# Two chains of pieces in the first stage, and a few input products of a 256-state scan moved from GpSimd to VectorE

## The chip, the core and the metric

The kernel runs on one core of a Trainium2 chip. The core has five engines, each with its own instruction queue that is worked off in order: TensorE (PE; its weight loads are listed as PEld), VectorE (DVE), ScalarE (ACT), GpSimd (POOL) and SyncE (SP), whose queue issues nearly all the DMA transfers here. Engines wait for each other through semaphores. All compute engines reach the on-chip memory SBUF; matrix products are written to PSUM, which DVE and ACT also read and write, and POOL does not use here. The metric is the device time of one execution in microseconds (us), lower is better.

## The reference

Four images of 128 channels and 64 x 64 pixels, all in float32, go through three parts.

1. *Ordering and a 16-state scan.* A group normalisation, then two depthwise 3 x 3 convolutions with Gelu and a channel gate between them give a score for each 4 x 4 patch; the 4096 pixels of each image are sorted by patch score. A selective scan with 256 channels of 16 states runs over the sorted pixels, and its result is put back in image order and added to the image.
2. *A 256-state scan.* Over the 4096 tokens of each image, with 256 channels `d` and 256 states `n`:

```python
deltaA = jnp.exp(jnp.einsum('bld,dn->bldn', delta, A))
deltaB = jnp.einsum('bld,bln->bldn', delta, Bv)
def step(state, inp):
    dA_i, dB_i, x_i, C_i = inp
    state = dA_i * state + dB_i * x_i[:, None, :]
    y = jnp.einsum('bdn,bn->bd', state, C_i)
    return (state, y)
```

3. *Spectral filters.* Causal convolutions of each image's tokens with 16 filters (in a plus and a minus form), each followed by a 128 x 128 matrix, plus a short autoregressive term. The matrices are sums over four branches, weighted by a softmax and by powers of `sigma`.

## The kernel before

The program has three stages in time: `layer0_front` (the ordering, until about 608 us), `layer0_scan` (the 16-state scan, until about 2850 us) and `layer1` (the 256-state scan with the spectral filters beside it, to the end).

**First stage, `layer0_front`.** A loop over the four images `b` (L118). For each: load the image into `xs`, take its statistics (L126), normalise it into the bordered tile `xg` (L144), copy it by patches into `xp1` (L149), transpose it in eight groups of four with statistics of each token (L164 to L172), take the powers `rs` and `r1` on POOL (L142, L176), and normalise the tokens `x1` on ACT (L183, 32 instructions). I call this the token part. Then the ordering part: the first convolution with Gelu (eight calls of `conv`: four of its nine taps are matmuls at L104, five are instructions on DVE at L106, of which the first reads PSUM and the others read only SBUF), the channel gate (L198 to L211), the second convolution (L215), scores (L225), ranks and the permutation matrix (L243 to L264), and the reordered tokens as matmuls with that matrix (L274, L277), stored to `xnt` (L278). `xs`, `xg`, `x1` and `f1` have one buffer each; `xp1` and the second convolution's result `f2` share one under the tag `patches`. Beside this the generator `spectral_weights` makes the spectral matrices: a softmax on the weights, the matrices `mue` from `M_u`, and then for each of 16 filters a load, four scalings on ACT (L677), three sums on POOL (L679) and two combinations on POOL (L695, L696), and stores. The loop advances it six times for each image but the first. In this stage the order of instructions on each engine is not the order in which the program emits them: a planner goes by emission as a priority and takes what is ready by its own estimate of time.

**Second stage, `layer0_scan`.** It is not touched. Its operations serve as prices: POOL forms inputs of 1024 elements per partition (L491), DVE scans them (L513) and multiplies the states, which lie in PSUM, by a tile in SBUF (L517).

**Third stage, `layer1`.** Here the order of instructions is written out by hand. There are 32 parts: four images of eight chunks of 512 tokens (`TS`). A part is 256 steps of the loop over `k` (L1253), one step for one channel `d`. States lie on the partitions, in two halves, so a step works on 128 x 1024 elements. Step `k` issues, in this order:

- `fetch` for step k + 8, every second step: delta of two channels, spread over all partitions by a DMA into `dlb` (L1140);
- `carry` for step k + 10, every 128 steps: two small products or sums on POOL (L1149, L1150) that bring in the state of the chunk before;
- `spread` for step k + 4, every second step (`VD` = 2 channels): POOL multiplies `u` by delta for both channels and writes tile `v` (L1155, three buffers); ACT puts in the first column (L1159);
- `lift` for step k + 1: ACT writes the decay factors as two exponentials into one of two PSUM tiles `da` (L1164);
- `scan` of step k: DVE's scan instruction over `da` and `v`, into `s` (L1167);
- every eight steps (`GD`) the list of six pieces of `contract`, of which one is taken at each of the next six steps: matmuls of the states with C into the PSUM tile `yp` (L1184) and ACT's copies out of it (L1190);
- one piece of the side work `beside` (the output of the part before, and the projections of the part after). A piece of kind `mm` (matmuls into `middle()`) is taken only at step 6 of eight and its evacuation (`post`) at step 7. `middle()` and `yp` share a single PSUM buffer, of which the eight steps are the timetable;
- spectral convolutions on PE up to a fixed number of columns per step (L1113, L1055), with ACT's copies (L1125).

Of the kernel before, what the change touches and what calls it, by code (L numbers as in the profile page):

```python
# [15 lines left out]
NB = 4  # L16
L = 4096
# [6 lines left out]
def layer0_front(ctx: ExitStack, tc, ident, half, w, x, xnt, perm_t, pqd, mud):  # L24
# [9 lines left out]
    pm = ctx.enter_context(tc.tile_pool(name="a_pm", bufs=4, space=PSUM))  # L34
# [83 lines left out]
    for b in range(NB):  # L118

        xs = xp.tile([128, L], F32, tag="xs", name="xs")  # L120
        nc.sync.dma_start(xs, x[b])
        for _ in range(6 if b else 0):
            next(matrices, None)
# [4 lines left out]
        nc.vector.bn_aggr(mv, st)  # L128

# [12 lines left out]
        nc.gpsimd.tensor_tensor(rs, sq, half[:, 0:1], ALU.pow)  # L142
        xg, inside = bordered("xg")
# [3 lines left out]
        xp1 = xp.tile([128, L], F32, tag="patches", name="xp1")  # L147
        for oy in range(4):
            nc.scalar.copy(  # L149
                by_patch(xp1, oy), inside[:, oy::4, :].rearrange("c py (px ox) -> c py px ox", ox=4)  # L150
            )


        x1 = xp.tile([128, 2, 16, 128], F32, tag="x1", name="x1")
# [5 lines left out]
        for h in range(2):  # L160
            for oy in range(4):
                tp = pm.tile([128, 4, 128], F32, tag="mm", name="tp")
                for ox in range(4):
                    nc.tensor.transpose(tp[:, ox, :], patches[:, h, 4 * oy + ox, :], ident)  # L164
                o4 = bass.ts(oy, 4)
                nc.vector.tensor_tensor(x1[:, h, o4, :], tp, pe[:, h, o4, :], ALU.add)
                for o in range(4):
                    nc.vector.bn_stats(stx[:, h, 4 * oy + o, :], tp[:, o, :])
                    nc.vector.bn_stats(st1[:, h, 4 * oy + o, :], x1[:, h, 4 * oy + o, :])
            for o in range(16):  # L170
                nc.vector.bn_aggr(mvx[:, h, o, :], stx[:, h, o, :])
                nc.vector.bn_aggr(mv1[:, h, o, :], st1[:, h, o, :])  # L172
# [8 lines left out]
        for h in range(2):  # L181
            for o in range(16):
                nc.scalar.activation(  # L183
                    x1[:, h, o, :], x1[:, h, o, :], AF.Identity, bias=m1[:, h, o : o + 1],
                    scale=r1[:, h, o : o + 1],
                )
# [4 lines left out]
        for i in range(8):  # L191
            h, oy = divmod(i, 4)
            nc.scalar.activation(
                inside1[:, 32 * h + oy : 32 * h + oy + 29 : 4, :], conv(xg, d1, w1, h, oy), AF.Gelu, bias=b1,
                accum_out=sums[:, i : i + 1],
            )
        mean = sm.tile([128, 1], F32, tag="mean", name="mean")
# [9 lines left out]
        nc.scalar.activation(ca, cap, AF.Sigmoid)  # L207
        d2b = xp.tile([128, PT, 128], F32, tag="d2b", name="d2b")
# [3 lines left out]
        f2 = xp.tile([128, L], F32, tag="patches", name="f2")  # L212
        for i in range(8):
# [4 lines left out]
            )  # L218

# [3 lines left out]
        for h in range(2):  # L223
            for o in range(16):
                nc.tensor.matmul(  # L225
                    sc[:, h, o : o + 1], fpatch[:, h, o, :], head,
                    start=True, stop=True,
                )
        s1 = sm.tile([128, 2, 16], F32, tag="s1", name="s1")
# [8 lines left out]

# [9 lines left out]
        for h in range(2):  # L248
# [10 lines left out]
            nc.vector.tensor_scalar(perm[:, h, :], index, more, None, ALU.is_equal)  # L259
        for h in range(2):  # L260
# [3 lines left out]
            nc.vector.tensor_copy(perm_t[:, b, h, :], tp.rearrange("p k j -> p (k j)"))  # L264


        xn = xp.tile([128, 3 + L], F32, tag="xn", name="xn")
        nc.vector.memset(xn[:, 0:3], 0.0)
        ranked = xn[:, 3:].rearrange("c (r o) -> c o r", o=16)
        for o in range(0, 16, 2):  # L270
# [6 lines left out]
            nc.scalar.activation(ranked[:, o : o + 2, :], ps, AF.Identity, bias=nb, scale=ng)  # L277
        nc.sync.dma_start(xnt[b], xn)  # L278

# [346 lines left out]
def spectral_weights(ctx, tc, sigma, m_u, m_plus, m_minus, log_w, gumbel, pqd, mud):  # L626
# [21 lines left out]
    tot = cp.tile([128, 1], F32, name="tot")  # L648
    nc.scalar.activation(soft, lw, AF.Exp, accum_out=tot)
# [31 lines left out]
    mu = mp.tile([128, 4, 3, 128], F32, name="mu", bufs=1)  # L681
    for i in range(4):
        nc.sync.dma_start(mu[:, i], m_u[i].rearrange("k d e -> d k e"))
    mue = mp.tile([128, 4, 3, 128], F32, name="mue", bufs=1)
    branch_sums(lambda r: mue[:, r], lambda i: mu[:, i], lambda i: wt[:, i : i + 1])
    nc.sync.dma_start(mud, mue)
    yield
    for k in range(NK):
        raw = mp.tile([128, 2, 4, 128], F32, tag="raw", name="raw")
        nc.sync.dma_start(raw[:, 0], m_plus[:, k].rearrange("i d e -> d i e"))  # L690
        nc.sync.dma_start(raw[:, 1], m_minus[:, k].rearrange("i d e -> d i e"))
        sums = mp.tile([128, 2, 4, 128], F32, tag="sums", name="sums")
# [23 lines left out]
def layer1(ctx: ExitStack, tc, ident, half, weights, phi, pqd, mud, x, omd, permd, x2, x3, out):  # L716
# [435 lines left out]
    def spread(d, dl, ready):  # L1152
# [3 lines left out]
            v[:, :, :, 1:], ready[0][:, :, 1:].unsqueeze(1).broadcast_to((128, VD, 2, TS - 1)),  # L1156
            dl[:, :, 1:].unsqueeze(2).broadcast_to((128, VD, 2, TS - 1)), ALU.mult,
        )
        nc.scalar.copy(v[:, :, :, 0], ready[5][:, :, bass.ds(d, VD)].rearrange("p h d -> p d h"))  # L1159
        return v  # L1160

# [66 lines left out]
    side, kind = None, None  # L1228
# [24 lines left out]
    for k in range(-10, steps):  # L1253
# [8 lines left out]
        if 0 <= j < steps and j % VD == 0:  # L1262
            vs[j // VD] = spread(j % 256, dls[j // VD], ready[j // 256])
# [21 lines left out]
        if kind == "free" or (kind == "mm" and at_step == 6) or (kind == "post" and at_step == 7):  # L1285
            kind = next(side, None)
        if at_step == GD - 1:
# [100 lines left out]
```

## Time and profile before

| what | us |
| --- | --- |
| three runs | 21599.78, 21605.29 (median), 21611.06 |
| profiled execution, its own time | 21607.92 |
| span of that execution, first to last instruction | 21606.2 |
| first stage, to the issue of the last `xnt` store | 607.7 |
| third stage, first scan to end | about 2859 to 21606 |

In the page's groups a line gives source line, engine, operation, output and inputs, partitions x elements, count, then busy time and the mean in ns of one, then idle time of the engine just before these instructions and what ended it. The chain of waits runs back from the last instruction to what released each one. Consecutive instructions of DVE or POOL overlap by some tens of nanoseconds when the next one waits for nothing, so that the distance between starts is a little shorter than a duration. A chunk of the third stage is 256 scans; counted from the first scan of one to the first of the next it takes 576 to 583 us. POOL's, DVE's and ACT's busy time in the stretch from 2880 to 21540 us are 18503.58, 18308.82 and 14178.81.

### The profile page before, as it was taken

What the parts mean: (1) busy time and instruction counts of PE and PEld (TensorE: products, weight loads), DVE (VectorE), ACT (ScalarE), POOL (GpSimd) and SP (SyncE); (2) the same over time, 40 slices, a digit from 0 to 9 for tenths busy, and PEclk for the clock granted to TensorE, in tenths of its full rate; (3) what the DMA queues carried; (4) which work ended last, traced back from release to release, by engine and by line L of the source; (5) the groups of instructions that cost most, each with busy time, mean ns of one, the idle gap of its engine ahead of it and who ended that gap; (6) DMA issues with size and microseconds to landing.
All of it is one profiled execution on the core that took longest, in us unless ns stands there. A gap on an engine that the chain in (4) does not pass through costs nothing.

```text
span 21606.2 us, 294251 instructions
## 1 busy us (share of the span) xinstructions
PE 17698.4 (82%) x99308; PEld 7770.7 (36%) x99308; DVE 20631.8 (95%) x11807; ACT 16015.2 (74%) x29548; POOL 20268.9 (94%) x5679
## 2 busy tenths in 40 slices
PE   6788854564858888886858999599999999999997
PEld 3344421231323333342323344243434434334434
DVE  6788889999999999999999999999999999999996
ACT  3677767777777777777777777787877777788875
POOL 2677789999999999999999999999999999999996
PEclk7999976676979999997979999699999999999999
DMA  1455544554656776665656777577777777777776
GB/s 68 112 140 140 140 150 151 170 181 160 216 173 218 219 222 218 220 214 186 211 178 218 227 236 235 169 236 232 236 230 228 232 232 231 231 231 229 228 229 187
DMA packets 2497355, 4302.23 MB, mean 199 GB/s; under 512 B 803256, under 2 KB 1320160, under 8 KB 2492768
## 3 DMA queue, kind: packets, MB, share of 16 engines
q1 hardware_dynamic: 2495840, 4283.40, 63.9%
q8 instruction: 784, 12.85, 0.2%
q14 instruction: 731, 5.99, 0.1%
HBM read 3658.98 MB, written 623.38 MB: 198 GB/s over the span
## 4 chain that ended last, share of the span: by engine, by line
DVE 47%; POOL 22%; PE 13%; ACT 8%; issue 6%; DMA 3%; SPq 0%; DVEq 0%; POOLq 0%; ACTq 0%
DVE s L1167 40%; POOL v L1155 21%; PE conv L1113 5%; ACT da L1164 5%; DVE states L513 3%; PE yp L1184 2%; DVE p L517 1%; PE fin L1055 1%; ACT f L505 1%; DMA dlb<-delta 1%; PE y L529 1%; DMA strip<-in_phi 1%; PE mm L422 1%; DMA yd<-ye 0%; PE conv L104 0%
## 5 line engine op out<-in xcount | busy, mean ns | idle before, releaser
L1155 POOL TENSOR_TENSOR v<-u,dlb 128x2044 f32<-128x2044 f32 x4096 | 18381.6, 4552 | 78.1 <-DMA dlb<-delta 68.3
L1167 DVE TENSOR_TENSOR_SCAN s<-da,v 128x1024 f32<-128x1024 f32 x8192 | 18134.6, 2272 | 249.2 <-ACT da L1164 124.8
L1164 ACT ACTIVATE da<-dlb,at 128x511 f32<-128x511 f32 x16384 | 11303.8, 690 | 2143.1 <-DVE s L1167 1688.3
L1113 PE MATMUL conv<-strip,tok 128*128 128x512 f32 (+3 forms) x20480 | 8656.1, 550 | 59.3 <-DMA strip<-in_phi 58.9
L1184 PE MATMUL yp<-s,c 128*32 128x256 f32 x65536 | 4952.4, 431 | 2709.5 <-DVE s L1167 1432.2
L1113 PEld LDWEIGHTS conv<-strip,tok 128*128 128x128 f32 x20480 | 3676.8, 192 | 4144.2 <-issue 3708.3
L1184 PEld LDWEIGHTS yp<-s,c 128*32 128x32 f32 x65536 | 1963.0, 120 | 6485.6 <-issue 1834.3
L1159 ACT COPY v<-vf 128x4 f32<-128x4 f32 x4096 | 814.6, 199 | 2128.6 <-DVE s L1167 2098.4
L1055 PE MATMUL fin<-conved,pq 128*128 128x512 f32 (+1 forms) x3968 | 1799.7, 546 | 16.2 <-ACT sum L1076 8.9
L491 POOL TENSOR_TENSOR v<-dx,bcb 128x1024 f32<-128x1024 f32 x512 | 1207.2, 2358 | 431.2 <-DVE states L513 427.0
L513 DVE TENSOR_TENSOR_SCAN states<-f,v 128x1024 f32<-128x1024 f32 x512 | 1175.9, 2297 | 175.9 <-ACT f L505 126.1
L505 ACT ACTIVATE f<-dt,an 128x255 f32<-128x255 f32 x2048 | 973.6, 476 | 420.9 <-DVE states L513 370.2
L1190 ACT COPY ye<-yp 128x512 f32<-128x512 f32 x2048 | 1185.9, 579 | 27.0 <-PE yp L1184 26.2
L1125 ACT COPY conved<-conv 128x512 f32<-128x512 f32 (+1 forms) x1728 | 986.6, 571 | 213.8 <-PE conv L1113 212.1
L529 PE MATMUL y<-p,ident 128*128 128x512 f32 x2048 | 1005.8, 620 | 154.2 <-DVE p L517 149.2
L1055 PEld LDWEIGHTS fin<-conved,pq 128*128 128x128 f32 x3968 | 669.8, 194 | 394.8 <-issue 284.0
L517 DVE TENSOR_TENSOR p<-states,bcb 128x1024 f32<-128x1024 f32 x512 | 627.0, 1225 | 39.3 <-PE y L529 0.5
L529 PEld LDWEIGHTS y<-p,ident 128*128 128x128 f32 x2048 | 368.8, 195 | 685.4 <-issue 356.0
L422 PE MATMUL mm<-ow,yg 128*32 128x128 f32 x2048 | 278.1, 294 | 107.0 <-ACT om L426 105.3
L422 PEld LDWEIGHTS mm<-ow,yg 128*32 128x32 f32 x2048 | 233.8, 138 | 212.0 <-ACT om L426 128.4
L356 PE MATMUL mm<-xin,taps 128*128 128x512 f32 x512 | 237.6, 608 | 27.2 <-issue 13.8
L398 POOL TENSOR_TENSOR e<-e,e 128x1024 f32<-128x1024 f32 x32 | 75.1, 2346 | 186.3 <-DMA bcb<-bcd 150.6
(240 smaller groups left out, 5851.1 us busy)
## 6 DMA issues: line engine op xcount, KB each, us to landing
dlb<-delta SPq DMA_DIRECT2D x4096, 512.0 KB, 4.1
strip<-in_phi SPq DMA_DIRECT2D x1536, 448.0 KB, 4.7
yd<-ye SPq DMA_DIRECT2D x2048, 256.0 KB, 4.0
strip<-in_phi SPq DMA_DIRECT2D x1088, 256.0 KB, 4.3
bcb<-bcd SPq DMA_DIRECT2D x1024, 256.0 KB, 4.1
pq<-pqd SPq DMA_DIRECT2D x1472, 64.0 KB, 3.7
yt<-yd SPq DMA_DIRECT2D x4096, 4.0 KB, 3.4
pq<-pqd SPq DMA_DIRECT2D x256, 128.0 KB, 3.8
```

Of the source, the lines that this page charges most:

```text
L491: nc.gpsimd.tensor_tensor(v, ready[n][2][:, :, bass.ts(i, SUB)].unsqueeze(1).broadcast_to((128, 2, 2, SUB)), bc[:, 0].unsqueeze(2).broadca ...
L505: nc.scalar.activation(factors[j % 2][:, a, k, 1:], ready[n][1][:, k, SUB * i + 1 : SUB * i + SUB], AF.Exp, scale=an[:, k, 2 * g + a : 2 * ...
L513: nc.vector.tensor_tensor_scan(states.rearrange(flat), factors[j % 2].rearrange(flat), v.rearrange(flat), 0.0, ALU.mult, ALU.add)
L529: nc.tensor.matmul(t.rearrange("p k t -> p (k t)"), ident, p[:, a].rearrange("p k t -> p (k t)"), start=g == 0 and a == 0, stop=False, ski ...
L1055: nc.tensor.matmul(fin[:, bass.ds(c0, w)], pq[:, n, :], u[:, bass.ds(c0, w)], start=begin and n == 0, stop=end and not partly, skip_group_ ...
L1113: nc.tensor.matmul(ps[:, skip:], tok[:, 1 - r if side else r, j, :], strip[:, bass.ds(c0 - lo, TS - skip)], start=which == 0 and j == js[0 ...
L1125: nc.scalar.copy(u[:, cols], ps[:, cols])
L1155: nc.gpsimd.tensor_tensor(v[:, :, :, 1:], ready[0][:, :, 1:].unsqueeze(1).broadcast_to((128, VD, 2, TS - 1)), dl[:, :, 1:].unsqueeze(2).br ...
L1164: nc.scalar.activation(da[:, h, 1:], dl[:, d % VD, 1:], AF.Exp, scale=at[:, h, d : d + 1])
L1167: nc.vector.tensor_tensor_scan(s[:, d % GD].rearrange("p h t -> p (h t)"), da.rearrange("p h t -> p (h t)"), v[:, d % VD].rearrange("p h t ...
L1184: nc.tensor.matmul(yp[i // 2][bass.ts(q, 32), i % 2], c[:, h, t], s[:, :, h, t], start=h == 0, stop=h == 1)
L1190: nc.scalar.copy(ye, yp[j].rearrange("p i d t -> p i t d"))
```

## The change

*First stage.* The loop body is split into two generators, `tokens(b)` (the token part, returning `xg`, `x1` and small tiles) and `ordered(b, ...)` (the rest, with the normalisation of `x1` in eight pieces of four instructions after each piece of the first convolution). A driver emits the tokens of image 0, and then for each image pieces of its ordering in turn with pieces of the tokens of the next image and steps of the spectral matrices: five steps of those for each image. `xp1` and `f2` have a buffer each, `x1` has two, `xn` takes the buffer of `xs`, and the PSUM pool of convolutions and transposes has six buffers in place of four. `spectral_weights` pauses before the softmax, handles `M_u` in three pieces by lag in place of one tile, and fetches the matrices of one filter ahead.

*Third stage.* At steps 118 and 246 of each part (`k % 128 == 118`), `spread` has POOL form only the first of the two channels. A new generator `relief` makes the other: at step 6 of eight ACT copies its delta from `dlb` into `middle()`, a PSUM tile, and at step 7, after that step's scan, DVE multiplies `u` by it into `v` (128 x 2 x 511 elements). A side piece of kind `mm` that would stand at that step 6 waits for the next group of eight.

```diff
-    pm = ctx.enter_context(tc.tile_pool(name="a_pm", bufs=4, space=PSUM))
+    pm = ctx.enter_context(tc.tile_pool(name="a_pm", bufs=6, space=PSUM))
...
-    for b in range(NB):
-        xs = xp.tile([128, L], F32, tag="xs", name="xs")
+    def tokens(b):
+        xs = xp.tile([128, 3 + L], F32, tag="xs", name="xs")[:, 0:L]
         nc.sync.dma_start(xs, x[b])
-        for _ in range(6 if b else 0):
-            next(matrices, None)
+        yield
...
-        xp1 = xp.tile([128, L], F32, tag="patches", name="xp1")
+        xp1 = xp.tile([128, L], F32, tag="xp1", name="xp1")
...
-        x1 = xp.tile([128, 2, 16, 128], F32, tag="x1", name="x1")
+        x1 = xp.tile([128, 2, 16, 128], F32, tag="x1", name="x1", bufs=2)
...
-        for h in range(2):
-            for o in range(16):
-                nc.scalar.activation(
-                    x1[:, h, o, :], x1[:, h, o, :], AF.Identity, bias=m1[:, h, o : o + 1],
-                    scale=r1[:, h, o : o + 1],
-                )
+        return xg, x1, mvx, r1, m1
+
+    def ordered(b, xg, x1, mvx, r1, m1):
...
+            for o in range(4 * i, 4 * i + 4):
+                h, o = divmod(o, 16)
+                nc.scalar.activation(
+                    x1[:, h, o, :], x1[:, h, o, :], AF.Identity, bias=m1[:, h, o : o + 1],
+                    scale=r1[:, h, o : o + 1],
+                )
+            yield
...
-        f2 = xp.tile([128, L], F32, tag="patches", name="f2")
+        f2 = xp.tile([128, L], F32, tag="f2", name="f2")
...
-        xn = xp.tile([128, 3 + L], F32, tag="xn", name="xn")
+        xn = xp.tile([128, 3 + L], F32, tag="xs", name="xn")
...
+    first = Pieces(tokens(0))
+    first.go()
+    for b in range(NB):
+        rest = Pieces(ordered(b, *first.result))
+        first = Pieces(tokens(b + 1)) if b + 1 < NB else Pieces(iter(()))
+        first.go(1)
+        for _ in range(4):
+            rest.go(2)
+            next(matrices, None)
+        first.go(1)
+        rest.go(2)
+        first.go(1)
+        rest.go(4)
+        first.go(1)
+        next(matrices, None)
+        rest.go(6)
+        for n in (1, 1, 1, 1, 1, 1, 2, 2):
+            first.go(1)
+            rest.go(n)
+        first.go()
+        rest.go()
...
+    for k in range(3):
+        raw = mp.tile([128, 2, 4, 128], F32, tag="raw", name="mu")[:, 0]
+        nc.sync.dma_start(raw, m_u[:, k].rearrange("i d e -> d i e"))
+        sums = mp.tile([128, 2, 4, 128], F32, tag="sums", name="mue")[:, 0]
+        branch_sums(lambda r: sums[:, r], lambda i: raw[:, i], lambda i: wt[:, i : i + 1])
+        nc.sync.dma_start(mud[:, :, k], sums)
...
+    ahead = fetch(0)
+    yield
+    for k in range(NK):
+        raw, ahead = ahead, fetch(k + 1) if k + 1 < NK else None
...
-    def spread(d, dl, ready):
+    def spread(d, dl, ready, n):
         v = wk.tile([128, VD, 2, TS], F32, tag="v", name="v", bufs=3)
         nc.gpsimd.tensor_tensor(
-            v[:, :, :, 1:], ready[0][:, :, 1:].unsqueeze(1).broadcast_to((128, VD, 2, TS - 1)),
-            dl[:, :, 1:].unsqueeze(2).broadcast_to((128, VD, 2, TS - 1)), ALU.mult,
+            v[:, 0:n, :, 1:], ready[0][:, :, 1:].unsqueeze(1).broadcast_to((128, n, 2, TS - 1)),
+            dl[:, 0:n, 1:].unsqueeze(2).broadcast_to((128, n, 2, TS - 1)), ALU.mult,
         )
...
+    def relief(v, dl, ready):
+        ps = middle()
+        nc.scalar.copy(ps, dl[:, VD - 1, :])
+        yield
+        nc.vector.tensor_tensor(
+            v[:, VD - 1, :, 1:], ready[0][:, :, 1:], ps[:, 1:].unsqueeze(1).broadcast_to((128, 2, TS - 1)),
+            ALU.mult,
+        )
+        yield
...
-            vs[j // VD] = spread(j % 256, dls[j // VD], ready[j // 256])
+            mine = k % 128 == 118 and kind != "post"
+            vs[j // VD] = spread(j % 256, dls[j // VD], ready[j // 256], VD - mine)
+            if mine:
+                helping = relief(vs[j // VD], dls[j // VD], ready[j // 256])
...
-        if kind == "free" or (kind == "mm" and at_step == 6) or (kind == "post" and at_step == 7):
+        if kind == "free" or (kind == "mm" and at_step == 6 and not helping) or (kind == "post" and at_step == 7):
             kind = next(side, None)
+        if helping and at_step >= 6:
+            next(helping)
+            helping = helping if at_step == 6 else None
```

## The prediction

> **What bounds the kernel now.** I read the page's shares and its chain of waits first, then the groups, then busy time by stage, then order in time inside one stage.
>
> ```profile
> PE 17698.4 (82%) x99308; PEld 7770.7 (36%) x99308; DVE 20631.8 (95%) x11807; ACT 16015.2 (74%) x29548; POOL 20268.9 (94%) x5679
> DVE 47%; POOL 22%; PE 13%; ACT 8%; issue 6%; DMA 3%; SPq 0%; DVEq 0%; POOLq 0%; ACTq 0%
> L1155 POOL TENSOR_TENSOR v<-u,dlb 128x2044 f32<-128x2044 f32 x4096 | 18381.6, 4552 | 78.1 <-DMA dlb<-delta 68.3
> L1167 DVE TENSOR_TENSOR_SCAN s<-da,v 128x1024 f32<-128x1024 f32 x8192 | 18134.6, 2272 | 249.2 <-ACT da L1164 124.8
> L491 POOL TENSOR_TENSOR v<-dx,bcb 128x1024 f32<-128x1024 f32 x512 | 1207.2, 2358 | 431.2 <-DVE states L513 427.0
> L517 DVE TENSOR_TENSOR p<-states,bcb 128x1024 f32<-128x1024 f32 x512 | 627.0, 1225 | 39.3 <-PE y L529 0.5
> ```
>
> DVE and POOL look equally busy, and the chain runs through both. The rows of stretches part them (columns: stretch, length, then PE, PEld, DVE, ACT and POOL busy, clock, DMA share, GB/s).
>
> ```profile
> 60.00:200.00 140.00, 80.51 (x239) 50.31 (x237) 98.19 (x130) 67.55 (x138) 96.67 (x83) 0.72 0.36 118
> 200.00:335.00 135.00, 100.31 (x306) 61.17 (x306) 92.41 (x268) 44.16 (x76) 6.00 (x2) 0.81 0.08 32
> 7494.00:8073.00 579.00, 505.09 (x2920) 204.68 (x2924) 573.11 (x285) 432.11 (x798) 578.77 (x136) 0.98 0.71 221
> 2880.00:21540.00 18660.00, 15426.81 (x92198) 6618.99 (x92191) 18308.82 (x9039) 14178.81 (x26210) 18503.58 (x4329) 0.91 0.68 212
> ```
>
> In a chunk of the 256-state scan (third row, 256 steps in 579 us) POOL works 578.77 us: it never rests. The instructions of DVE in order of time show what its 573 hides:
>
> ```profile
> 12168.59 0.67 DVE L927 TENSOR_TENSOR t<-mm,t 128x512 f32<-128x512 f32 x1
> 12169.17 17.55 DVE L1167 TENSOR_TENSOR_SCAN s<-da,v 128x1024 f32<-128x1024 f32 x8
> 12205.30 19.73 DVE L1167 TENSOR_TENSOR_SCAN s<-da,v 128x1024 f32<-128x1024 f32 x9
> 12241.76 53.89 DVE L1167 TENSOR_TENSOR_SCAN s<-da,v 128x1024 f32<-128x1024 f32 x24 [0.43 <-POOL v L1155]
> ```
>
> Nine scans with inputs in stock take 19.73 us, so (19.73 - 2.27) / 8 = 2.18 us a step. The 24 that follow POOL take (53.89 - 2.27) / 23 = 2.244, which is POOL's pace: 18381.6 / 4096 / 2 = 2.244. Back-to-back scans overlap; waiting ones lose that, and busy time cannot see it. So POOL is the bound here, and DVE's own need per chunk is 256 x 2.1825 = 558.7, plus its small work. L927 starts 0.58 us before the next scan although it lasts 0.67: seven such (4.1), two groups of eight statistics instructions (12224.95 to 12225.99 on the same timeline, 2.1 together) and four of L880 (0.28 each, 1.0), 7.2 in all, plus ACT's 124.8 / 32 = 3.9. Together 569.8, some 10 us under POOL.
>
> In the first stage no engine is full (second row above: PE 100, DVE 92 of 135 us): a chain binds it.
>
> ```profile
> 54.36 5.45 POOL r L176
> 228.53 5.45 POOL r L176
> 363.17 5.45 POOL r L176
> 499.41 5.41 POOL r L176
> 607.68 8.01 DMA xnt<-xn
> ```
>
> L176 stands near the end of an image's token part. Its distances are 174.2, 134.6 and 136.2 us, and after the last, 108.3 us to the final store. So ordering an image alone takes 108, and 27 us of each period are the next image's tokens in series. The first period has 39 more: the chain there runs through L677, L679, L695 and L696, the spectral matrices (POOL busy 96.67 of 140).
>
> **The change, part by part.**
>
> Spreads. 64 of 4096 lose half. POOL's full one steps by 4.488 us. The half is bounded by 2.24 (half) and 2.36 (L491, 1024 elements); I take 2.29, nearer the second since that row has the size. Saved: 2.2 x 2 = 4.4 us a chunk. POOL's need falls from 579.9 (128 x 4.488 = 574.4, L1149/L1150 twice 1.5, L787/L788 twice 1.24) to 575.5.
>
> The product on DVE. 1022 elements, one operand in PSUM like L517 (1.225, less the 0.09 overlap that L927 shows: 1.14). Upper bound: if it shared a port with POOL it would stretch as the two-SBUF-operand instructions did in the first image:
>
> ```profile
> L106 DVE SCALAR_TENSOR_TENSOR sum<-f,w2b,sum 128x512 f32<-128x512 f32 x32 | 41.2, 1299 | 0.8
> L106 DVE SCALAR_TENSOR_TENSOR sum<-f,w2b,conv 128x512 f32<-128x512 f32 x8 | 5.9, 737 | 9.0 <-PE conv L104 6.1 <-ACT f L215 2.9
> ```
>
> While POOL worked (60 to 200 us), the SBUF-only form took 1299 ns (750 in the second image) but the form with an operand in PSUM 737. The new product is of the second kind: 1.14, with 2.6 as its bound. DVE's need: 569.8 + 2.3 = 572.1, under POOL's 575.5; at 2.6 it is 575.0, level. So POOL stays the bound and each chunk falls by 4.4: 32 x 4.4 = 141. I take off half a microsecond a chunk (16), because DVE's reserve shrinks from 10 to 3.4 us: after the relief POOL leads by 4.36 + 1.14 - 1.5 (carry, same step) - 2.29 = 1.7 us, and with three v buffers it must stop at about one pair, 4.4; a statistics group (1.04) or ACT hold-up can add up to that. **Third stage: -125**, bounds -141 and 0.
>
> A rule that speaks against this: the Trainium skill (Perfetto Trace Analysis, Identifying the Most-Contended Engine) takes the engine of highest occupancy as the bottleneck. By it DVE, 95% to 94%, is the bound and the change loads it with 64 x 1.14 = 73 us, which would be the sum for this stage. The step of 2.18 against 2.244 overrules it for me.
>
> ACT's copy of delta into PSUM: 64 x 0.58 (L1190, same size) = 37 us, beside ACT's idle (14179 busy of 18660); its price without that cover is those 37. The added wait: the product waits for that copy. Behind it on DVE stand scan 120 and all later; PE's yp of the next group waits for it too (one PSUM buffer), ACT's exponentials for the scan. The copy stands behind two exponentials (1.38), perhaps a conved copy (0.57) and 0.2 for the v column: done some 2.7 us after scan 117, while DVE reaches the product after two scans, 4.36. No wait, 1.6 us in hand.
>
> The matmul piece that gives up its slot comes 8 steps (18 us) later. The projection ends (last L882) some 437 us into a chunk of 580, so this is hidden; uncovered it would be 18 us a chunk.
>
> First stage. The tokens of images 1 to 3 move beside the ordering of the image before: up to 3 x 27 = 81. DVE has room: 92.4 busy of 135, its gaps lying under the score matmuls and the ranked ones (13.66 and 14.41 on the chain of the last image) and the gate. The normalisation L183, 12.43 us in front of the first Gelu on that chain, is cut into eights between Gelus: up to 10 per image, though DVE, then nearly full, returns most; I count 9 in all. More PSUM and x1 buffers only make this possible. The matrices stay in series with image 0: their instructions were emitted with images 1 to 3 and yet ran at 76 to 180 us, so where they are emitted hardly sets when they run. If they do spread, up to 39 more; then the two-operand L106 of other images stretch instead, which gives part back. **First stage: -90**, bounds 0 and -150.
>
> SP's queue: the M_u loads and store become three of each, same bytes; matrix loads go one ahead; xs now shares its buffer with xn, so an image's load waits for a store: 8.0 + 9.2 (median landing) = 17 us, against the first convolution's 27 us of DVE work (40 x 0.67) before it is needed. Without that cover, 17 us for each of two images. POOL's two powers (0.56 and 5.4) can stand behind a matrix (6.4): 6 us late on a token chain of 27 within 108. The added pause before the softmax moves 103 us of POOL work that has the whole stage.
>
> **Sum.** The profiled run is 21607.9 (span 21606.2): - 125 - 90 = 21393. The median is 2.6 lower: 21390.
>
> **Rivals.**
> - In-order queues keep the tokens in series (for: DVE's statistics wait for transposes, which would queue behind PE's convolution matmuls; against: PE idles 35 of 135 us). Third stage only: 21605 - 125 = 21480.
> - The product waits for POOL's half of the same tile: 1.5 + 2.29 = 3.8 more per event, DVE 569.8 + 2 x 4.9 = 579.6 per chunk, and the relief is worth nothing: 21605 - 90 = 21515. Against: different columns. For: tile v is shared by three engines.
> - The matrices spread and L183 hides: -150 - 125: 21330.
> - Slower: the wait for ACT's copy, at scan 120. To eat the first stage's 90 us a chunk must reach 582.7, so (582.7 - 569.8) / 2 = 6.5 us per event, a wait of 5.3. ACT's longest recorded wait for PE in this stage is 4.1 us (conved), less 1.6 in hand: 2.5. If every wait were 8 us: 569.8 + 2 x 9.1 = 588, +8.2 x 32 - 90: 21777.
> - It does nothing measurable: both rivals one and two: 21605.
>
> **How the numbers follow.** Forecast 0.58 (own range 21350 to 21440), tokens in series 0.12, wait for POOL 0.10, everything better 0.12, slower 0.05, nothing 0.03. A measurement of this kernel tells about 0.2% (43 us) from no change. Faster 0.92, same 0.03, slower 0.05. The range 21325 to 21515 leaves out the last two cases and the far end of the better one.
>
> **What will show it.** Right: a chunk of about 576 us with POOL still without rest; 64 DVE products near 1.2 us with no gap before them; L176 distances near 110 us after the first and the final xnt store near 520. Wrong: a gap ahead of the product ended by POOL or ACT; POOL idle, ended by DVE; half spreads well above 2.4; L176 distances still 135.

## The result, and the profile after

The changed kernel takes 21437.16 us (median of 4 runs, 21428.15 to 21444.59), the kernel before 21605.13 beside it (4 runs; 21605.33 over the 11 of the next round): a ratio of 0.9922, 95% interval [0.9909, 0.9934], so 0.66 to 0.91% faster. The forecast was 21390, in a range of 21325 to 21515. The sign and the place of both gains were right; 47 us of the predicted 215 did not come. The profiled execution took 21431.38 us, with a span of 21429.6.

| stretch of the profiled execution | before | after | difference | predicted |
|---|---|---|---|---|
| start to last xnt store issued | 607.7 | 542.7 | -65.0 | -90 |
| last store to first scan of stage two | 73.5 | 73.4 | 0 | 0 |
| stage two (first to last 16-state scan) | 2103.7 | 2109.7 | +6.0 | 0 |
| to the first 256-state scan | 74.0 | 75.6 | +1.6 | 0 |
| 31 chunks of the 256-state scan, mean | 580.04 | 576.26 | -3.78 each, -117.4 | -3.9 each |
| last chunk | 591.9 | 586.5 | -5.4 | -3.9 |
| last scan to the end of VectorE's last sum | 170.3 | 174.1 | +3.8 | 0 |

So the two stages that were changed lost 65.0 and 122.8 us against 90 and 125. The three stretches with a plus, 11.4 us together, have the same code before and after. Over the thirteen profiles told of here, stage two ran from 2102.9 to 2113.2 us and the end from 167.3 to 174.1, whatever was changed elsewhere; I read these 11 us as scatter. That is not shown for all of them: the two profiles with the old first stage have 2103.7 and 2102.9 us in stage two, the eleven with the new one 2103.7 to 2113.2, so a few of the 6.0 us may belong to the change.

The page's shares and its chain of waits by engine, of the kernel after:

```profile
PE 17672.7 (82%) x99308; PEld 7756.7 (36%) x99308; DVE 20566.6 (96%) x11871; ACT 16044.5 (75%) x29620; POOL 20134.2 (94%) x5685
DVE 57%; PE 14%; POOL 9%; ACT 9%; issue 8%; DMA 3%; SPq 0%; DVEq 0%; POOLq 0%; ACTq 0%
```

DVE is busier than POOL by two points where it was by one, and that says little. The chain says more: POOL held 22% of it before and holds 9% now, DVE 47% and now 57%.

The groups of the third stage, split by shape (columns: count, then total us, mean ns, and idle time just before):

```profile
L1212 POOL TENSOR_TENSOR v<-u,dlb 128x2044 f32<-128x2044 f32 x4032 | 18096.9, 4552 | 91.7 <-DMA dlb<-delta 66.0 <-DVE s L1235 24.8
L1235 DVE TENSOR_TENSOR_SCAN s<-da,v 128x1024 f32<-128x1024 f32 x8192 | 18006.6, 2264 | 188.3 <-ACT da L1232 130.3 <-POOL v L1212 42.2
L1212 POOL TENSOR_TENSOR v<-u,dlb 128x1022 f32<-128x1022 f32 x64 | 151.0, 2359 | 0.0
L1224 DVE TENSOR_TENSOR v<-u,mm 128x1022 f32<-128x1022 f32 x64 | 76.2, 1190 | 0.0
```

64 spreads are halves of 2359 ns, and VectorE makes the other halves in 1190 ns each. The last column of L1224 is 0.0: not once in 64 times did VectorE stand idle ahead of the product, neither for ScalarE's copy nor for POOL. DVE's scans had 249.2 us of idle time before them and have 188.3. One of the products, in DVE's order of time (start, length):

```profile
7665.77 13.19 DVE L1235 TENSOR_TENSOR_SCAN s<-da,v 128x1024 f32<-128x1024 f32 x6 [2.40 <-ACT da L1232]
7678.89 1.19 DVE L1224 TENSOR_TENSOR v<-u,mm 128x1022 f32<-128x1022 f32 x1
7680.00 8.82 DVE L1235 TENSOR_TENSOR_SCAN s<-da,v 128x1024 f32<-128x1024 f32 x4
```

It starts 0.07 us before the scans ahead of it end, and the next scan starts 1.11 us after it: 1.11 is what it costs. Then the rows of stretches (columns as in the prediction): a period of the first stage, and a chunk.

```profile
200.00:320.00 120.00, 96.62 (x307) 60.63 (x306) 92.80 (x268) 43.80 (x79) 5.99 (x2) 0.83 0.09 35
7410.00:7986.00 576.00, 505.86 (x2933) 205.01 (x2931) 571.81 (x287) 433.74 (x800) 574.39 (x135) 0.97 0.73 223
```

In the first row DVE does in 120 us what it did in 135 (92.8 against 92.4), and still has 27 us of gaps. In a chunk of 576 us POOL rests 1.6 and DVE 4.2: the two are level. Of the waits in the third stage, only those between the two engines (total us, how often, longest), before and after:

```profile
DVE s L1167 <- POOL v L1155: 85.2, 90, 3.1
POOL v L1155 <- DVE s L1167: 9.7, 9, 2.2
```

```profile
DVE s L1235 <- POOL v L1212: 34.1, 38, 3.4
POOL v L1212 <- DVE s L1235: 24.8, 27, 3.5
```

VectorE's wait for POOL fell by more than half, and POOL waits for VectorE two and a half times as much as it did.

The first stage, by the chain of waits in order of time:

```profile
54.59 5.45 POOL r L179
191.16 5.46 POOL r L179
310.27 5.45 POOL r L179
429.81 5.43 POOL r L179
542.73 8.57 DMA xnt<-xn
```

The distances are 136.6, 119.1 and 119.5 us, and 112.9 to the last store (before: 174.2, 134.6, 136.2, 108.3). The prediction said near 110 after the first, with the last store near 520; its 27 us an image make 147 of the first. The 112.9 is not the ordering alone: L179 of the last image now starts 13 us before the store of the image before (443.2). From store to store the last image takes 99.6 us.

### The profile page after: what moved, and what is told of

It is laid out like the page before. It is cut to its first block, busy times and chain, and to the rows that moved or that the text cites. A ratio compares the mean times of both kernels' runs of the same rounds, so it can differ in the third digit from the quotient of the medians.

```text
span 21429.6 us, 294489 instructions
## 1 busy us (share of the span) xinstructions
PE 17672.7 (82%) x99308; PEld 7756.7 (36%) x99308; DVE 20566.6 (96%) x11871; ACT 16044.5 (75%) x29620; POOL 20134.2 (94%) x5685
## 4 chain that ended last, share of the span: by engine, by line
DVE 57%; PE 14%; POOL 9%; ACT 9%; issue 8%; DMA 3%; SPq 0%; DVEq 0%; POOLq 0%; ACTq 0%
DVE s L1235 50%; POOL v L1212 8%; PE conv L1169 6%; ACT da L1232 5%; DVE states L562 3%; PE yp L1252 3%; DVE p L566 2%; PE fin L1111 1%; ACT f L554 1%; PE y L578 1%; DMA strip<-in_phi 1%; DMA dlb<-delta 1%; PE mm L471 1%; PE conv L104 0%; DVE v L1224 0%
## 5 line engine op out<-in xcount | busy, mean ns | idle before, releaser
L1212 POOL TENSOR_TENSOR v<-u,dlb 128x2044 f32<-128x2044 f32 (+1 forms) x4096 | 18244.4, 4517 | 91.7 <-DMA dlb<-delta 66.0
L1235 DVE TENSOR_TENSOR_SCAN s<-da,v 128x1024 f32<-128x1024 f32 x8192 | 18006.6, 2264 | 188.3 <-ACT da L1232 130.3
L1252 PE MATMUL yp<-s,c 128*32 128x256 f32 x65536 | 4957.0, 432 | 2616.2 <-DVE s L1235 1136.7
```

The costliest lines, as they stand in the source:

```text
L1212: nc.gpsimd.tensor_tensor(v[:, 0:n, :, 1:], ready[0][:, :, 1:].unsqueeze(1).broadcast_to((128, n, 2, TS - 1)), dl[:, 0:n, 1:].unsqueeze(2) ...
L1235: nc.vector.tensor_tensor_scan(s[:, d % GD].rearrange("p h t -> p (h t)"), da.rearrange("p h t -> p (h t)"), v[:, d % VD].rearrange("p h t ...
L1252: nc.tensor.matmul(yp[i // 2][bass.ts(q, 32), i % 2], c[:, h, t], s[:, :, h, t], start=h == 0, stop=h == 1)
```

## The experiments

Theory after the result: (a) the third stage went as predicted, VectorE relieving POOL until the two are level, and the PSUM copy is what makes that possible; (b) the first stage fell short because the next image's tokens are only half hidden: VectorE and TensorE execute them inside the ordering's own chain. Rivals: that the two parts hinder each other, that reading delta from PSUM doesn't matter, that more relief would give more, that the normalisation or the spectral matrices hold up the first stage.

### Each part alone

Kernel one is the kernel before with the relief of the third stage alone (the new spread, relief and the slot). Kernel two is the changed kernel without it:

```diff
-            mine = k % 128 == 118 and kind != "post"
-            vs[j // VD] = spread(j % 256, dls[j // VD], ready[j // 256], VD - mine)
-            if mine:
-                helping = relief(vs[j // VD], dls[j // VD], ready[j // 256])
+            vs[j // VD] = spread(j % 256, dls[j // VD], ready[j // 256])
```

> Only the third stage's part of the change; the first stage is as before. My theory (POOL's need per chunk sets the pace, the relief takes 4 us of it): third stage 123 us shorter, the first as before, so 21605 - 123 = 21482. Rival (part of what the third stage gained in the changed kernel came from starting earlier or from another state of buffers): a chunk differs from 576.3 us and the sum of both parts alone is not the whole.

> Only the first stage's part; no relief in the scan. My theory: the last xnt store at 543 us, chunks at 580, together 21605 - 55 = 21550 (65 less in the first stage, some 6 to 10 given back later). Rival (the two parts lean on each other): more or less than 40 to 65 us off.

The relief alone: 21489.79 (21486.81 to 21492.12), ratio 0.9945 [0.993, 0.996], 116 us under before; chunks of 576.36 us, last store at 607.4. The first stage alone: 21549.5 (8 runs, 21541.36 to 21557.67), ratio 0.9973 [0.9963, 0.9984], 56 us; chunks of 580.10, last store at 544.0. Together 171, and both at once gave 168: the parts add up and don't touch each other. What the first run also settles is which engine bound the third stage before: VectorE's work grew by 76 us and the kernel lost 116.

The rule that the prediction weighed, that the engine of highest occupancy is the bottleneck (the Trainium skill, Perfetto Trace Analysis, Identifying the Most-Contended Engine), would have made this run longer. The measurement decides against it: at 95 to 94% the shares did not order the two engines.

### Delta from SBUF in place of PSUM

```diff
-        ps = middle()
-        nc.scalar.copy(ps, dl[:, VD - 1, :])
         yield
         nc.vector.tensor_tensor(
-            v[:, VD - 1, :, 1:], ready[0][:, :, 1:], ps[:, 1:].unsqueeze(1).broadcast_to((128, 2, TS - 1)),
+            v[:, VD - 1, :, 1:], ready[0][:, :, 1:],
+            dl[:, VD - 1, 1:].unsqueeze(1).broadcast_to((128, 2, TS - 1)),
```

> As the changed kernel, but DVE reads delta from SBUF, so the product has two operands there, and ACT makes no copy. If the two-operand form shares a port with POOL, as the first stage's rows say, the product grows from 1.19 us to about 2 and the POOL spread beside it by up to 1 us: chunks 1 to 2.5 us longer, 21470 to 21515. Rival (where delta lies is of no account): product 1.19 us, time 21437 within 15.

21509.69 (21503.4 to 21511.58), ratio 0.9954 [0.9939, 0.9969]: 72 us over the changed kernel, so well over half of the relief's 116 is gone, although ScalarE's 64 copies are saved. Chunks take 578.81. The group of the products (63 of the 64, the last lies outside the stretch):

```profile
L1222 DVE TENSOR_TENSOR v<-u,dlb 128x1022 f32<-128x1022 f32 x63 | 153.3, 2433 | 0.0
```

The same product with both operands in SBUF takes 2517 ns on the mean of all 64 (median 2026, 1185 to 7926) where it took 1190 from PSUM, every time. The spreads of POOL beside it stretched too: 34 of the full ones took 5.08 to 5.52 us, where the longest in the changed kernel takes 4.70. The prediction's upper bound for the product, 2.6 us from the stretch of L106 in the first image, was thus near the right size for the wrong operand, and the operand in PSUM is what keeps the price at 1.19. The Trainium skill (SBUF — State Buffer, Who interferes with whom) says that a VectorE instruction with two SBUF inputs contends with a GpSimd one that reads SBUF, and that the port pair they share is an exclusive lock: whoever comes first has it for the whole instruction, and the other blocks fully. Both show here. POOL's half spread, VectorE's product and POOL's next spread, at one of the reliefs:

```profile
13486.59 2.37 POOL L1212 TENSOR_TENSOR v<-u,dlb 128x1022 f32<-128x1022 f32 x1
13487.11 2.93 DVE L1222 TENSOR_TENSOR v<-u,dlb 128x1022 f32<-128x1022 f32 x1
13488.92 5.50 POOL L1212 TENSOR_TENSOR v<-u,dlb 128x2044 f32<-128x2044 f32 x1
```

The product starts in the middle of the half spread and ends 1.08 us after it; the next spread ends 4.38 us after the product, although it was begun before. So it goes throughout: 63 of the 64 products end 1.08 to 1.11 us after the end of an instruction of POOL, and the one that meets none takes 1.20. So a product's length follows from where POOL stands when it starts: here 1.85 us were left, plus 1.08. The four of 7.85 to 7.93 us let two spreads pass, a half and a full one, before their turn; why they lost twice I did not find out.

### Twice as many reliefs

```diff
-            mine = k % 128 == 118 and kind != "post"
+            mine = k % 64 == 54 and kind != "post"
```

> As the changed kernel, but with a relief at every 64th step, four a chunk. Theory: after two reliefs DVE's own need (573.0 us a chunk, waits for POOL left out) is already close to POOL's 575.5; with four it is 573.0 + 2.2 = 575.2 and POOL's 571, so DVE binds and a chunk stays at 575 to 576.5: 21405 to 21440. Rival (POOL is still the whole bound): 4.2 us a chunk more off, 134 in all, 21303.

21434.46 (21430.22 to 21437.86), ratio 0.992 [0.9903, 0.9937]: the changed kernel's time. The waits between the two engines in the third stage now:

```profile
POOL v L1212 <- DVE s L1235: 102.0, 107, 5.6
DVE s L1235 <- POOL v L1212: 19.6, 15, 2.9
```

POOL waits for VectorE four times as long as with two reliefs, and the chunk stays at 576.56. POOL's need has fallen by another 4.4 us, to some 571, and the chunk did not follow: VectorE is the bound here, with its waits for ScalarE's exponentials (144.0 us in all, 130.3 with two reliefs). Two reliefs a chunk had already come to the balance point, so the 16 us that the prediction took off for VectorE's shrinking reserve had a reason.

### The normalisation tied to the gate

In the changed kernel, cutting the normalisation into eights in the text did not put it between the Gelus. ScalarE's order, second image:

```profile
204.31 6.62 ACT L199 ACTIVATE x<-x,m,r 128x128 f32<-128x128 f32 x17
210.95 1.28 ACT L193 ACT_TABLE_LOAD   x1
212.25 0.73 ACT L193 ACTIVATE f<-sum,b 128x512 f32<-128x512 f32 x1
```

26 of the 32 still stand ahead of the first Gelu, nine among the last copies of the image before (L291, from 196.86 to 203.29) and these 17 in one run, though in the text four come after each. This kernel makes them depend on the gate (a bias with zero times ca added), so that they can only run in the second convolution:

```diff
         nc.scalar.activation(ca, cap, AF.Sigmoid)
+        late = sm.tile([128, 2, 16], F32, tag="late", name="late")
+        nc.vector.tensor_scalar(late, m1, 0.0, ca, ALU.mult, ALU.mult)
+        nc.vector.tensor_tensor(late, late, m1, ALU.add)
...
                 conv(f1, d2b, w2b, h, oy).rearrange("c py (px ox) -> c py px ox", ox=4), AF.Gelu, bias=b2,
             )
+            for o in range(4 * i, 4 * i + 4):
+                h, o = divmod(o, 16)
+                nc.scalar.activation(
+                    x1[:, h, o, :], x1[:, h, o, :], AF.Identity, bias=late[:, h, o : o + 1],
+                    scale=r1[:, h, o : o + 1],
+                )
```

The same loop with bias=m1 is taken out of the first convolution.

> The changed kernel, with the 32 instructions that normalise x1 (L199, 0.39 us each) tied to the gate's result, so that they can't stand in front of the first Gelu of the first convolution; nothing else differs but two small VectorE instructions per image. Theory: in the changed kernel 17 of the 32 (6.5 us) and a table load (1.28 us) still hold up the first Gelu of images 1 to 3, and with it the Gelu chain; without them each image is 5 to 8 us shorter: final xnt store at 510 to 520 instead of 542.7, run 21405 to 21415. Rival: VectorE's taps (40 x 0.67 = 27 us, and the next image's statistics beside them) set the first convolution, so the Gelus catch up: at most 2 us per image, 21430 to 21437, store at 535 or later; and if the 12 us of normalisation now hold up the second convolution's Gelus, up to 12 us per image longer, 21485.

21422.58 (21413.44 to 21423.65), ratio 0.9912 [0.9897, 0.9926]. The L179 distances are 136.4, 116.7 and 119.4, and 109.5 to the last store, at 535.8: an image is 0.1 to 3.4 us shorter, not 5 to 8. VectorE's order in the changed kernel says why:

```profile
213.09 0.75 DVE L106 SCALAR_TENSOR_TENSOR sum<-xg,w,conv 128x512 f32<-128x512 f32 x1 [2.00 <-ACT f L193]
```

The late Gelus stop VectorE for 2.00 us only: with three sum buffers it works ahead, and from there its 40 taps of 0.75 us set the first convolution. The rival was right about the mechanism, though the run lies between the two forecasts. It is 15 to 21 us below the changed kernel's (21437.2, and 21443.4 in the last experiment), of which the store explains 7 to 12. The two profiled executions lie 7.7 us apart (21431.4 and 21423.7), 6.9 of them at the store, so I take the rest for scatter between executions.

### The matrices tied to image 0's score

A zero times image 0's score (hold[0]) is added to the logits, so no matrix can be made before that image is scored; the driver takes none of their steps beside image 0, and more beside the later ones.

```diff
+    zero = cp.tile([128, 1], F32, name="zero")
+    nc.vector.tensor_scalar(zero, hold[0], 0.0, None, ALU.mult)
+    nc.vector.tensor_scalar(lw, lw, zero, None, ALU.add)
     nc.scalar.activation(soft, lw, AF.Exp, accum_out=tot)
```

> The changed kernel, with the spectral matrices' softmax tied to image 0's score (score times zero is added to the logits), so that none of the matrices can run on GpSimd before image 0 is scored; they run beside images 1 to 3. Theory: the 17 us by which image 0's L179 distance (136.6) exceeds the later ones (119) are the two-operand L106 instructions stretched beside GpSimd's matrix work; the stretch goes wherever the matrices go, so the first distance falls to 116 to 122 and the next ones grow by as much together: run 21430 to 21445. Rival one: the matrices hold up image 0 by their burst at the start alone; spread, they cost less: first distance 116 to 122, others 119 to 122, run 21415 to 21425. Rival two: the matrices have nothing to do with it (first convolution starting cold, loads of the first weights): first distance stays 134 or more, run 21430 to 21445.

> Both edits: normalisation tied to the gate, matrices tied to image 0's score. If each of the two theories holds the time is that of the late normalisation alone, 21405 to 21415; if the matrices' rival one holds as well, 21390 to 21400; if the normalisation's rival holds, 21430 to 21440.

21444.2 (21440.2 to 21449.61), ratio 0.9923 [0.9908, 0.9938]. The distances are now 113.1, 151.6 and 121.5: image 0 is 23.5 us shorter and image 1 is 32.5 longer, the last store comes at 555.5. The second convolution's taps on VectorE, in the stretch of image 0 (60 to 180 us) and of image 1 (200 to 300 us) of the changed kernel:

```profile
L106 DVE SCALAR_TENSOR_TENSOR sum<-f,w2b,sum 128x512 f32<-128x512 f32 x32 | 40.6, 1280 | 0.7
L106 DVE SCALAR_TENSOR_TENSOR sum<-f,w2b,sum 128x512 f32<-128x512 f32 x32 | 23.5, 749 | 0.7
```

and of this kernel (60 to 160, and 190 to 305 us):

```profile
L106 DVE SCALAR_TENSOR_TENSOR sum<-f,w2b,sum 128x512 f32<-128x512 f32 x32 | 23.5, 749 | 0.7
L106 DVE SCALAR_TENSOR_TENSOR sum<-f,w2b,sum 128x512 f32<-128x512 f32 x32 | 39.6, 1251 | 0.7
```

The stretch has moved with the matrices, whole: 32 x 0.5 = 16 to 17 us. With the first convolution's taps, 918 ns on the mean in image 0 of the changed kernel and 746 in this one (32 of them, 5.5 us), that is 22.5 us, near the 23.5 that image 0 gains. Image 1 lost more than that, which the theory did not have: there the two convolutions' taps make some 22 of the 32.5 us, and the matrices' place in ScalarE's queue counts as well:

```profile
223.57 0.51 ACT L739 ACTIVATE sums<-raw,both 128x256 f32<-128x256 f32 x1 [8.98 <-DMA raw<-in_M_phi_minus]
223.98 0.71 ACT L194 ACTIVATE f<-sum,b 128x512 f32<-128x512 f32 x1
231.18 0.16 DVE L207 TENSOR_REDUCE mean<-sums 128x1 f32<-128x8 f32 x1 [7.28 <-ACT f L194]
```

A Gelu stands behind a scaling of the matrices that waits 8.98 us for its load, and VectorE then idles 7.28 us before the mean that the gate needs. So by size most of the matrices' price is the two-operand taps running beside POOL, and it is paid wherever the matrices run; no run separates it from ScalarE's queue, since both move together. They ran as one burst again (188 to 305 us), so whether a thin spread over three images would be cheaper isn't settled. Both edits together gave 21427.94 (21425.58 to 21430.74), ratio 0.9916 [0.9899, 0.9932], between the two and 2 us under the forecast for the normalisation's rival.

### Three images without their tokens

In this kernel images 1 to 3 use image 0's tokens (x1, its statistics, means and powers); of their own they have the load and the normalised image xg. Their statistics, group sums, powers, transposes and L168 to L178 are left out.

```diff
+        if b:
+            gm, rs, x1, mvx, r1, m1 = kept
+            xs = xp.tile([128, 3 + L], F32, tag="xs", name="xs")[:, 0:L]
+            nc.sync.dma_start(xs, x[b])
...
+            nc.vector.tensor_scalar(
+                inside, xs.rearrange("c (y x) -> c y x", x=64), gm, rs, ALU.subtract, ALU.mult
+            )
+            return xg, x1, mvx, r1, m1
```

> The changed kernel, in which images 1 to 3 take their tokens (x1, its statistics, means and powers) from image 0; of their own they keep the load and the normalised image xg. So their statistics (8 L126), group sums, POOL powers, transposes, L168 to L178 are left out of three images. Theory: in the changed kernel this work stands inside the ordering's own chain (5.5 us of L126 in the first convolution, where VectorE is full; 5 us of group sums and power ahead of the gate's d2b; 4 us of transposes among the score matmuls; 4 us of statistics in the sort; 1.5 among the ranked matmuls), and that is why a period is 119 and not 108: without it the final xnt store comes at 542.7 - 3 x (15 to 20) = 483 to 498, run 21375 to 21392. Rival: the ordering alone is slower than I read it (its buffers, the normalisation ahead of the first Gelu), and the tokens are hidden: store at 530 or later, run 21425 or more.

21387.76 (21384.5 to 21392.52), ratio 0.9899 [0.9882, 0.9915]: 49 us under the changed kernel. SyncE's store of each image (start, length), in this kernel:

```profile
198.43 0.32 SPq L307 DMA_DIRECT2D xnt<-xn  x1
301.11 0.32 SPq L307 DMA_DIRECT2D xnt<-xn  x1
403.59 0.32 SPq L307 DMA_DIRECT2D xnt<-xn  x1
503.17 0.32 SPq L307 DMA_DIRECT2D xnt<-xn  x1
```

and in the changed one:

```profile
204.53 0.32 SPq L293 DMA_DIRECT2D xnt<-xn  x1
323.65 0.32 SPq L293 DMA_DIRECT2D xnt<-xn  x1
443.18 0.32 SPq L293 DMA_DIRECT2D xnt<-xn  x1
542.73 0.32 SPq L293 DMA_DIRECT2D xnt<-xn  x1
```

An ordering with no tokens beside it takes 102.6 us from store to store, one with them 119.3. Before the change it was 134.6 to 136.4: so the tokens cost about 33 us a period in series, and 16.7 of them are still there. I had expected 15 to 20 three times; it came twice and 6.1 us in image 0, because the last image has no successor beside it: 39.6 us, store at 503.2 and not 483 to 498. It accounts for most of the 49 us (42.8 between the two profiled executions). Why image 0 gave 6.1 and not 16 I did not separate. Theory (b) holds. Where the half is, VectorE's order of time in the changed kernel shows:

```profile
217.31 1.41 DVE L106 SCALAR_TENSOR_TENSOR sum<-xg,w,sum 128x512 f32<-128x512 f32 x2
218.64 0.69 DVE L126 BATCH_NORM_STATS2 st<-xs 128x6 f32<-128x512 f32 x1
...
233.52 1.87 DVE L126 BATCH_NORM_STATS2 st<-xs 128x6 f32<-128x512 f32 x3
235.31 0.14 DVE L206 TENSOR_REDUCE mean<-sums 128x1 f32<-128x8 f32 x1
...
239.62 2.42 DVE L146 TENSOR_SCALAR xg<-xs,gm,rs 128x4096 f32<-128x4096 f32 x1 [0.66 <-POOL rs L143]
241.95 0.48 DVE L218 TENSOR_SCALAR d2b<-d,ca 128x512 f32<-128x512 f32 x1
...
247.68 0.75 DVE L106 SCALAR_TENSOR_TENSOR sum<-f,w2b,conv 128x512 f32<-128x512 f32 x1 [5.11 <-PE conv L104]
```

Eight L126 (5 us) lie between the taps of the first convolution, where VectorE does not rest after 213 us; the last three even stand ahead of the mean that the gate waits for. Then xg, with the group sums and POOL's power ahead of it, comes before d2b, for which TensorE waits: from mean to d2b 6.6 us, in the kernel without tokens 1.7. Behind d2b VectorE stands idle for 5.11 us, with nothing left to fill the gap. TensorE does the like among the scores:

```profile
271.69 3.41 PE L236 MATMUL sc<-head,f 128*128 128x1 f32 x16
274.96 0.68 PE L166 MATMUL tp<-ident,xp 128*128 128x128 f32 x4
275.48 3.52 PE L236 MATMUL sc<-head,f 128*128 128x1 f32 x16
```

17.8 us from the first score matmul to the last, 13.66 without transposes. The sort, from the score's scaling (L246) to the first transposed permutation (L277), takes 8.9 us among the tokens' statistics and 5.1 without. The four differences, 5, 4.9, 4.2 and 3.8, come to some 18, near the 16.7. The first two are put to the test below; the transposes and the sort are read from the trace only.

### The statistics tied to the gate

If that reading is right, the same work in VectorE's gap behind d2b costs less. On top of the late normalisation, the statistics' tile is first written with a product of ca, so that the eight L126 must follow the gate; group sums and xg are put after them in the text.

```diff
         st = sm.tile([128, 8, 6], F32, tag="st", name="st")
+        if b:
+            nc.vector.tensor_scalar(st, pe[:, 0, 0, 0:48].rearrange("p (q s) -> p q s", s=6), gates[-1], None, ALU.mult)
```

> The late normalisation (e5), with the next image's statistics (8 L126, 5.5 us) made to wait for the gate's result, so that they run in the 5 us that VectorE idles between d2b and the first matmuls of the second convolution; group sums, power and xg then come inside the second convolution. Theory: the first convolution is 5.5 us shorter and the gate 5 us, while 3.2 us of xg and group sums go into the second convolution: 6 to 7 us per period, three times: 21400 to 21406 against e5's 21422.6, store at 515 to 518 instead of 535.8. Rival: VectorE is full in the second convolution too, and ACT's four copies of xp and the transposes now come late, so that scores or sort wait for as much: store at 530 or later, 21417 or more.

21397.81 (21392.42 to 21407.82), ratio 0.9904 [0.9889, 0.9919]. VectorE's order of time at the same place:

```profile
225.65 0.16 DVE L204 TENSOR_REDUCE mean<-sums 128x1 f32<-128x8 f32 x1 [0.36 <-ACT f L197]
227.53 0.48 DVE L220 TENSOR_SCALAR d2b<-d,ca 128x512 f32<-128x512 f32 x1
...
228.44 4.84 DVE L130 BATCH_NORM_STATS2 st<-xs 128x6 f32<-128x512 f32 x8
233.41 0.75 DVE L106 SCALAR_TENSOR_TENSOR sum<-f,w2b,conv 128x512 f32<-128x512 f32 x1
```

Mean to d2b is 1.9 us, and the eight statistics (4.84) lie in the gap that was 5.11. The distances fall to 134.7, 107.4 and 112.1, the last store comes at 518.0. That is the 108 and the -90 of the forecast, reached by an edit that the change does not have.

Since this interval touches that of the changed kernel, both were run once more beside each other on one chip:

> The changed kernel, timed beside the kernel with the late statistics on one chip, because their intervals against the kernel before touch: 21428 to 21445.

> The kernel of e9 (statistics and normalisation tied to the gate) again, beside the changed one. If the shorter first stage alone (final xnt store 24.7 us earlier) is what it gains, it is 20 to 30 us under the changed kernel; more than that would have come by chance from later stages, whose code is the same.

21443.41 (21439.57 to 21450.05) and 21413.99 (21412.06 to 21417.16), with the kernel before at 21621.06: 29 us apart and no run of the one within those of the other. The last stores came at 547.7 and 520.1, 27.6 us apart, so the first stage accounts for the difference. This version beats both kernels. The changed kernel's own last store thus lies between 542.7 and 547.7 from one execution to another.

## Why the prediction was right or wrong

**Third stage, -125: right**, measured -122.8, and -116 for that part alone as a whole run. POOL was the bound, read from scans at 2.18 us with inputs in stock and 2.244 behind POOL. The half spread took 2.36 where I took 2.29 (0.14 us a chunk), and a chunk 576.26 against the 575.5 of POOL's need: 0.8 over, where I had taken off half a microsecond for VectorE's thin reserve. That the reserve was nearly gone is shown by four reliefs, which gave nothing more.

**The product, 1.14 us: right**, 1.19 long and 1.11 in effect; the bound of 2.6 is near what the SBUF form costs on the mean (2.52). That nearness is luck: the mean depends on where POOL's instructions stand when the product starts.

**The added wait: right.** No idle time ahead of any of the 64 products; TensorE's yp waited 241.9 us for them in all; that is hidden, since its idle time as a whole did not grow (2709.5 us before yp's matmuls before the change, 2616.2 after). So neither the rival of ScalarE's copy nor that of POOL's half occurred.

**The matmul slot, 18 us later: nothing seen**, as forecast: no chunk grew.

**First stage, -90: the sign right, the size wrong by 25.** The step that failed is "DVE has room: 92.4 busy of 135", with gaps under the score matmuls, the ranked ones and the gate, and with it "up to 3 x 27 = 81". The gaps are there, and remain: 27 us in each 120 after the change. But a gap is filled only by work that is ready when it opens and not put ahead of something urgent. The statistics were ready early and went into the first convolution, where VectorE is full; xg went ahead of d2b; the transposes went among the scores. Periods became 119, not 108. Leaving the tokens out gave 102.6, moving the statistics 107 to 112. The 27 itself, taken from the last image's 108.3, was too small: by the run without tokens it was about 33.

**The normalisation, up to 10 per image less what VectorE returns, 9 in all: not measured by itself.** It was hardly cut into eights: 26 of the 32 remained in front of the first Gelu. What that still cost is small, 2.0 us of VectorE's time an image, and tying all 32 to the gate brought the last store 6.9 us forward.

**Image 0, 147 by the same 27: wrong in the good direction**, 136.6. That the matrices stay beside image 0 and cost time there was right: the tied kernel moved the cost to image 1. Why image 0 gained 38 and not 27 I did not separate by a run.

**SP's queue, powers, the pause before the softmax: costed at nothing.** Little of it shows: an image's load after the store, costed at 17 us under cover, is on the chain once (6.57 and 7.72 us from 323.65), beside VectorE's taps, and VectorE waited 0.19 us for it.

Of the 38.4 us by which the profiled execution missed the working's 21393, 25 are the first stage, 2.2 the third, 11.4 the stretches with unchanged code.

## What to carry to other kernels

Between two engines at 94 and 95%, find the bound by the pace of back-to-back work with inputs in stock against the pace behind the other engine; relieve the slower one only until the two are level, and give the helper an operand outside SBUF if GpSimd works beside it. When a second chain is laid beside a first, count not the idle time but which piece of it is ready at each gap: work that becomes ready early is put into the full stretches, ahead of what the first chain waits for, and a false dependency on the event at which the gap opens is a cheap way to move it there.

## What the runs showed of the hardware that was not expected

With both operands in SBUF and POOL at work, one and the same VectorE product took anything from 1185 to 7926 ns; from PSUM it took 1174 to 1195. 63 of the 64 ended 1.08 to 1.11 us after the end of a GpSimd instruction, four of them after letting two spreads pass, and a full spread behind one was held up in its turn (5.5 us for 4.55). And 32 two-operand taps took 749 ns each without POOL's matrices, and 1251 to 1280 with them, in whichever image these ran, while the taps with one operand in PSUM stayed at 736 to 743.
